# Two GNN layers on one core: set-up reordered, with extra transposes and all adjacency parts ordered by GpSimd

## The chip, the core and the metric

The kernel runs on one core of a Trainium2 chip. A core has five engines that run beside each other, each with its own queue of instructions in a fixed order: TensorE (PE, matrix products and transposes, results in PSUM), VectorE (DVE), ScalarE (ACT), GpSimd (POOL) and SyncE (SP, here only a queue that starts DMAs). They wait for each other by semaphores. The metric is the device time of one execution in microseconds, the median of several runs.

## What is computed

Eight graphs of 2048 nodes with 256 features share one 2048 × 2048 adjacency matrix of zeros and ones (int32). Layer 0 is attention with four heads over chunks of 256 keys, layer 1 a graph attention; both have a layer norm and a ReLU ahead and are added to their input.

```python
# layer 0, on h = relu(layernorm(x))
scores = einsum('bhnd,bhjcd->bhnjc', q, kc) / sqrt(Dh)      # 4 heads, 8 chunks of 256 keys
scores = clip(scores, -10.0, 10.0)
scores = where(mask == 0, -10.0, scores)                    # mask = adjacency
attn = softmax(scores, axis=-1)                             # within each chunk
ctx = einsum('bhnjc,bhjcd->bhnd', attn, vc)                 # summed over the chunks
x = x + layernorm(ctx @ Wo.T + bo + h) * gamma + beta
# layer 1, on h = relu(layernorm(x)) @ W
e = where(adj == 0, NEG_INF, leaky_relu(e_src[:, :, None] + e_dst[:, None, :]))
x = x + relu(softmax(e) @ h)
```

## The kernel before

Nodes are handled in blocks of 512 (`NB`; four blocks, `NNB`), each of four tiles of 128. For each graph, layer 0 runs 32 attention steps (`Attention.STEPS`: four blocks of queries, each with eight chunks of keys), and layer 1 follows. The order of all instructions is written out by hand; each engine takes its own in the order of the program. The set-up, which is what the change touches, runs once, ahead of the steps of the first graph.

**The adjacency matrix in the set-up.** The mask is kept in turned form as int8 bounds: clipping the logits from below by a constant and from above by a bound that is 80 or -80 does both the clip and the mask (`Attention.clip`, L530). To make the bounds, the matrix is read in 32 parts, each 128 rows of queries by half of the keys (1024 columns of int32, 512 KB). 24 of them (`nearest`, L1016) are done in the set-up, the other eight (`all_parts[-8:]`) beside the first attention steps. Each part passes through five stations:

- `load_rows` (L258): a DMA on SP's queue into one of four buffers (tile `rows`). The load of part i + 4 is issued after `find` of part i, L1031.
- `missing_of` (L267), called by `find`: VectorE compares with zero and writes bf16 (tile `z`), L277. A first half (`half` = 0) is written directly in the order of keys that the kernel uses. For a second half (`aside`, L271) VectorE writes in plain order, and GpSimd copies it into the other order, L281. `z` has five buffers, which it shares with the attention weights `e`.
- `turn_missing` (L284): eight transposes on TensorE into PSUM (`ps_z`), L292.
- `keep_bounds` (L295): ScalarE turns them into int8 bounds, L303. Blocks 0 and 1 (parts 0 to 15) stay in SBUF (`bounds[nb]`).
- Parts 16 to 23 (block 2) go to `bound_part` and from there to DRAM by a DMA that GpSimd issues at once, L306. `bound_part` has four tiles in turn (`part_tags`: r, o4, r, prod), so each tile is used twice in the set-up, and its second use waits until the first is landed.

`turn_missing` and `keep_bounds` together are `bound` (L1037).

**The projections in the set-up.** `proj.stats`, `power`, `shift` and `norm` make the normalised input of a block (VectorE, ScalarE), `turn` transposes it on TensorE (L375) and copies it to `hT` (L408 on VectorE, L410 on ScalarE), `qk` makes queries (part 0) and keys (part 1) of a block (L434; copied by ScalarE, L438), `values` its values (L448; L453 on VectorE). `turn_weight` transposes a weight (L250, L251). The set-up ends with `att.early(0)` to `early(3)`: logits of the first attention step and the first logits of the second (L490), clips (L530), exponentials (L539) and the first addition of exponentials, on GpSimd (L545). In the steps themselves, `begin` and `end` issue the products with the values (L506), the sums (L518) and the rest.

**PSUM.** Three rings of two tiles each: `s` (logits, and the projections of blocks 0 to 2), `n` and `t`, which take turns in the set-up (`ps_m`, `turn_missing`). A new tile of a ring waits until its forerunner but one has been read.

The lines that matter are these:

```python
for nb in range(NNB - 1):                 # L1047
    i = 6 * nb
    proj.qk(nb, 0, ps_h)
    find(i + 2, i + 3)
    bound(i, i + 1)
    proj.qk(nb, 1, ps_h)
    find(i + 4, i + 5)
    bound(i + 2, i + 3)
    proj.turn(nb + 1, 0)
    proj.values(nb)
    find(i + 6, i + 7)
    bound(i + 4, i + 5)
```

Of the kernel before, what the change touches and what calls it, by code (L numbers as in the profile page):

```python
# [17 lines left out]
P = 128  # L18
# [10 lines left out]
def gnn_two_layers(  # L29
# [18 lines left out]
    nc = tc.nc  # L48
# [7 lines left out]
    TB = NB // P  # L56
# [14 lines left out]
    def ps_n():  # L71
        return ps.tile([P, 512], F32, tag="n", name="ps_n")

    def ps_t():
        return ps.tile([P, 512], F32, tag="t", name="ps_t")
# [4 lines left out]
    def ps_m():  # L80
        if turn_about[0]:
            turn_about[1] += 1
            if turn_about[1] % 2:
                return ps_n()
        return ps_t()
# [9 lines left out]
    ident = const.tile([P, P], F32, name="ident")  # L95
# [19 lines left out]
    bound_d = [kept.tile([P, NT, NB], I8, name=f"bound_d{nb}") for nb in range(NNB)]  # L115
# [74 lines left out]
    def row_bcast(src, name):  # L190
        t = const.tile([P, F], F32, name=name)
        nc.sync.dma_start(t, row(src))
        return t
# [51 lines left out]
    def turn_weight(raw, wT):  # L245
        pt = ps_m()
        for di in range(FC):
            for do in range(FC):
                k = di * FC + do
                nc.tensor.transpose(pt[:, k * P:(k + 1) * P], raw[:, do, di * P:(di + 1) * P], ident)  # L250
        nc.vector.tensor_copy(wT.rearrange("p c f -> p (c f)"), pt)  # L251

    HALF = N // 2
    in_setup = [True]
# [3 lines left out]
    def load_rows(t, half):  # L258
        rows = xpool.tile([P, HALF], I32, tag="x", name="rows", bufs=NNB)
        of_block = adj[t // TB * NB:(t // TB + 1) * NB, half * HALF:(half + 1) * HALF]  # L260
        nc.sync.dma_start(rows, of_block.rearrange("(p t) k -> p t k", t=TB)[:, t % TB, :])
        return rows

    def in_blocks(keys):
        return keys.rearrange("p (k b t) -> p k t b", t=TB, b=Q)

    def missing_of(rows, t, half):  # L267

        tag = "e" if in_setup[0] else "hn"
        z = work.tile([P, 2 if in_setup[0] else 1, HALF], BF16, tag=tag, name="z", bufs=5)  # L270
        aside = in_setup[0] and half  # L271
        apart = dict(t=TB, b=Q)
        if aside:
            src, dst = rows, z[:, 1, :]
        else:
            src, dst = in_blocks(rows), z[:, 0, :].rearrange("p (k t b) -> p k t b", **apart)
        nc.vector.tensor_scalar(  # L277
            dst, src, 0.0, 0.0, op0=ALU.is_equal, op1=ALU.add, accum_out=missing[:, t, half:half + 1],
        )
        if aside:  # L280
            nc.gpsimd.tensor_copy(z[:, 0, :].rearrange("p (k t b) -> p k t b", **apart), in_blocks(z[:, 1, :]))  # L281
        return z[:, 0, :]

    def turn_missing(z):  # L284
        tag = "t"
        if turn_about[0]:
            turn_about[1] += 1
            if turn_about[1] % 2:
                tag = "n"
        pt = ps.tile([P, 8, P], BF16, tag=tag, name="ps_z")  # L290
        for k in range(8):
            nc.tensor.transpose(pt[:, k, :], z[:, k * P:(k + 1) * P], ident_b)  # L292
        return pt

    def keep_bounds(pt, t, half):  # L295

        nb, rows, cols = t // TB, slice(half * 8, (half + 1) * 8), slice((t % TB) * P, (t % TB + 1) * P)
        if nb in bounds:
            dst = bounds[nb][:, rows, cols]
        else:  # L300
            tag = part_tags[(2 * t + half) % 4] if in_setup[0] else "r"
            dst = work.tile([P, 8, P], I8, tag=tag, name="bound_part", bufs=2 if tag == "r" else 1)
        nc.scalar.activation(dst, pt, AF.Copy, scale=-2.0 * CLIP * SC, bias=CLIP * SC)  # L303
        if nb not in bounds:
            queue = nc.gpsimd if in_setup[0] else nc.scalar
            queue.dma_start(bound_d[nb][:, rows, cols], dst)  # L306

    def find_lone():
        nc.vector.tensor_reduce(lone, missing, AX.X, ALU.add)
# [4 lines left out]
    def adjacency(parts):  # L314


        def load(i):
            rows[i] = load_rows(*parts[i])

        def find(i):  # L320
            found[i] = missing_of(rows.pop(i), *parts[i])

        def turn(i):
            found[i] = turn_missing(found[i])

        def keep(i):
            keep_bounds(found.pop(i), *parts[i])

        finds = [9, 11, 15, 17, 21, 23, 29, 31]
        turns = [12, 12, 18, 18, 26, 26, 32, 32]  # L330
        todo = {}
        for i, (f, t) in enumerate(zip(finds, turns)):
            todo.setdefault(f - 6, []).append(lambda i=i: load(i))
            todo.setdefault(f, []).append(lambda i=i: find(i))
            todo.setdefault(t, []).append(pe(lambda i=i: turn(i)))
            todo.setdefault(t + 1, []).append(first(lambda i=i: keep(i)))
        return todo
# [122 lines left out]
    def fence(before, after):  # L460

        nop = nc.sync.nop()
        for x in before:
            tc.add_manual_dep(nop.ins, x.ins.name, SYNC, reason="both write one bank of PSUM")
        for x in after:
            tc.add_manual_dep(x.ins, nop.ins.name, SYNC, reason="both write one bank of PSUM")


    class Attention:
# [127 lines left out]
        def begin(self, f, pieces=()):  # L597

            self.run(pieces, "first")
            if self.has(f - 3):  # L600
                made = {}
                for kt in range(KT):
                    for half, c in ((0, 0), (1, 1)):
                        made.setdefault(c, []).extend(self.values(f - 3, half, c, kt))
                for c in range(2):
                    fence(self.before.pop((f - 3, c)), made[c])
            if self.has(f - 1):
                self.clip(f - 1, 0)
            if self.has(f - 3):
                self.invert(f - 3)  # L610
            if self.has(f - 2):
                self.exponentials(f - 2, 3)
            if self.has(f - 1):
                self.exponentials(f - 1, 0)
            self.run(pieces, "pe")
            if self.has(f - 1):
                for kt in range(KT):
                    self.logits(f - 1, 1, kt)
                    self.logits(f - 1, 2, kt)
            if self.has(f - 3):  # L620
                self.scale(f - 3, 0)
                self.scale(f - 3, 1)
            if self.has(f - 2):
                self.add(f - 2, 1)
            if self.has(f - 3):
                self.gather(f - 3)
            self.rest = pieces
# [377 lines left out]
    proj = Projection(0)  # L1005
# [9 lines left out]
    all_parts = [(t, half) for t in range(NT) for half in range(2)]  # L1015
    nearest = all_parts[:-8]  # L1016
    rows = {i: load_rows(*nearest[i]) for i in range(4)}
    proj.stats(0, range(TB))
    proj.power(0)
    turn_weight(raws["q"], wqT)  # L1020
    proj.shift(0)
    turn_weight(raws["k"], wkT)
    turn_weight(raws["v"], wvT)
    proj.norm(0, 0)
    proj.norm(0, 1)
    proj.load(2)
# [4 lines left out]
    def find(*parts):  # L1031
        for i in parts:
            found[i] = missing_of(rows.pop(i), *nearest[i])
            if i + 4 < len(nearest):
                rows[i + 4] = load_rows(*nearest[i + 4])

    def bound(*parts):  # L1037
        for i in parts:
            keep_bounds(turn_missing(found.pop(i)), *nearest[i])
# [4 lines left out]
    proj.power(1)  # L1044
    proj.shift(1)
    find(0, 1)
# [3 lines that stand above are left out]
        if nb == 0:  # L1050
            proj.norm(1, 0)
            proj.norm(1, 1)
            proj.load(3)
        find(i + 2, i + 3)
        bound(i, i + 1)
        proj.qk(nb, 1, ps_h)
        find(i + 4, i + 5)
        bound(i + 2, i + 3)
        if nb + 2 < NNB:
            proj.stats(nb + 2, range(TB))  # L1060
            proj.power(nb + 2)
            proj.shift(nb + 2)
        proj.turn(nb + 1, 0)
        proj.turn(nb + 1, 1)
        if nb + 2 < NNB:
            proj.norm(nb + 2, 0)
            proj.norm(nb + 2, 1)
        proj.values(nb)
        find(i + 6, i + 7)
        bound(i + 4, i + 5)  # L1070
        if nb == 0:
            bo_r = row_bcast(bo, "bo_r")
            gamma_r = row_bcast(gamma, "gamma_r")
            beta_r = row_bcast(beta, "beta_r")
    att = Attention(proj)
    att.early(0)
    proj.qk(NNB - 1, 0)
    att.early(1)
    find(20, 21)
# [2 lines left out]
    att.early(2)  # L1082
    bound(20, 21)
    find(22, 23)
    bound(22, 23)
    proj.values(NNB - 1)
    att.early(3)
    in_setup[0] = False

    def layer1_weight():  # L1090
# [27 lines left out]
    for b in range(B):  # L1118
# [205 lines left out]
        for i, (nb, j4) in enumerate(pieces1):  # L1324
# [34 lines left out]
            if ahead and i == len(pieces1) - 4:  # L1359
                att = Attention(ahead)  # L1360
# [38 lines left out]
```

## Time and profile before

| what | value |
|---|---|
| median of 3 runs | 3558.47 us (3555.39 to 3564.36) |
| the profiled execution | 3563.89 us |
| its span | 3562.1 us |
| granted clock, mean | 0.998 |
| L277 on VectorE, 24 parts, set-up | 1210 to 2184 ns |
| L281 on GpSimd, 12 copies, set-up | 1086 to 1133 ns |
| L292 on TensorE, 8 transposes of a part | 0.62 us |
| L303 on ScalarE, one part | 1.02 us |
| L306, one send on GpSimd's queue | 0.9 us, 2.7 to 9.7 us from issue to landing |
| rows, 512 KB, issue to landing | 5.4 us median |

Times within the execution count from the start of the span. The profile names each group by its line, engine, operation and tiles; "x8" is the number of instructions in it (an f32 matrix product shows as two). A figure in brackets is the time that the engine stood idle before, with what ended it. An instruction's duration on TensorE includes its latency, so a dense row of matmuls is best measured from the start of one group to the start of the next.

### The profile page before, as it was taken

Reading aid. Unit: us, or ns where it says so; the run is one execution under the profiler, and the core shown is the slowest. Engines: PE = TensorE matmul, PEld = TensorE weight load, DVE = VectorE, ACT = ScalarE, POOL = GpSimd, SP = SyncE. Lnnn points to the kernel's source line nnn. Section 1 sums busy time; section 2 is a strip of 40 time slices with the busy share of each in tenths; the row PEclk is TensorE's granted clock in tenths of the full one; section 3 lists DMA queues with packets and bytes.
Section 4 is the critical chain, followed back from the end, with each engine's and each line's share of the span. In section 5 each row is a group of like instructions: output and inputs, shape, how many; then the busy total and the mean of one; then the engine's idle time right before and its main releaser. Section 6 shows DMA issues by size and latency. Waiting matters only on the chain.

```text
span 3562.1 us, 104433 instructions
## 1 busy us (share of the span) xinstructions
PE 3527.6 (99%) x46080; PEld 2183.0 (61%) x46080; DVE 2639.0 (74%) x3979; ACT 1947.4 (55%) x2961; POOL 1808.9 (51%) x1182
## 2 busy tenths in 40 slices
PE   8999999999999999999999999999999999999999
PEld 5455785557755577555775557655586555855568
DVE  7888677867678676786767867678586785757866
ACT  6677426763267633676236762367624766147750
POOL 2688016870278702786037850378404784048731
PEclk9999999999999999999999999999999999999999
DMA  7545423444234441344423444234442434124321
GB/s 234 119 107 134 87 74 85 91 113 91 80 79 85 123 95 60 85 96 109 92 66 85 97 110 91 71 79 91 120 103 55 91 81 118 57 55 91 85 69 48
DMA packets 169111, 329.74 MB, mean 93 GB/s; under 512 B 35664, under 2 KB 97360, under 8 KB 160464
## 3 DMA queue, kind: packets, MB, share of 16 engines
q1 hardware_dynamic: 127696, 203.51, 19.2%
q0 software_dynamic: 32640, 118.50, 18.0%
q8 instruction: 360, 5.90, 0.7%
q10 hardware_dynamic: 8320, 1.05, 0.2%
q14 instruction: 95, 0.78, 0.1%
HBM read 154.14 MB, written 51.43 MB: 58 GB/s over the span
## 4 chain that ended last, share of the span: by engine, by line
PE 97%; DVE 1%; DMA 1%; ACT 1%; issue 0%; POOL 0%; ACTq 0%; DVEq 0%; POOLq 0%; SPq 0%
PE ps_s L490 25%; PE ps_n L506 24%; PE ps_s L963 12%; PE ps_t L518 7%; PE ps_n L963 6%; PE ps_t L963 6%; PE ps_t L714 2%; PE ps_t L434 2%; PE ps_n L434 2%; PE ps_s L434 2%; PE ps_t L814 2%; PE ps_n L814 2%; PE ps_t L448 1%; PE ps_n L448 1%; DVE z L277 0%
## 5 line engine op out<-in xcount | busy, mean ns | idle before, releaser
L530 DVE SCALAR_TENSOR_TENSOR e<-ps_s,bound 128x1024 f32<-128x1024 f32 x1024 | 1224.1, 1220 | 404.0 <-PE ps_s L490 400.6
L545 POOL TENSOR_TENSOR both<-e 128x1024 f32<-128x1024 f32 x512 | 1219.8, 2407 | 571.1 <-PE ps_t L518 355.6
L490 PE MATMUL ps_s<-q,k 64*32 64x512 f32 x16384 | 1431.8, 590 | 1.5 <-DVE e L530 1.4
L539 ACT ACTIVATE e<-e 128x1024 f32<-128x1024 f32 x1024 | 1050.6, 1050 | 481.1 <-DVE e L530 462.7
L506 PE MATMUL ps_n<-e,v 64*32 64x512 f32 x16384 | 1224.9, 591 | 2.4 <-DVE prod L560 2.4
L506 PEld LDWEIGHTS ps_n<-e,v 64*32 64x32 f32 x16384 | 460.9, 107 | 473.1 <-issue 384.1
L490 PEld LDWEIGHTS ps_s<-q,k 64*32 64x32 f32 x16384 | 459.5, 106 | 448.6 <-issue 331.2
L518 PE MATMUL ps_t<-both,ones 64*32 64x512 f32 x4096 | 537.9, 592 | 0.1
L963 PE MATMUL ps_s<-g,w 128*128 128x257 f32 x2048 | 447.8, 380 | 0.0
L963 PEld LDWEIGHTS ps_s<-g,w 128*128 128x128 f32 x2048 | 388.8, 190 | 56.3
L560 DVE TENSOR_TENSOR prod<-ps_n,rz 128x512 f32<-128x512 f32 x448 | 288.5, 686 | 162.8 <-PE ps_n L506 96.1
L986 POOL TENSOR_TENSOR x<-x,r 128x256 f32<-128x256 f32 x124 | 90.7, 745 | 466.2 <-ACT r L984 465.4
L946 DVE SCALAR_TENSOR_TENSOR w<-bound,w 128x1024 f32<-128x1024 int8 x256 | 314.7, 1229 | 8.7
L354 POOL TENSOR_TENSOR krn<-krn,mv 128x4 f32<-128x4 f32 x28 | 6.8, 242 | 575.4 <-DVE w L940 575.4
L963 PE MATMUL ps_n<-g,w 128*128 128x257 f32 x1024 | 292.4, 382 | 0.0
L963 PE MATMUL ps_t<-g,w 128*128 128x257 f32 x1024 | 289.7, 380 | 0.0
L550 ACT ACTIVATE rz<-ps_t 128x512 f32<-128x512 f32 x256 | 152.6, 596 | 229.4 <-PE ps_t L518 201.5
L940 DVE TENSOR_SCALAR w<-src,cd 128x512 f32<-128x512 f32 x512 | 263.1, 556 | 7.0 <-ACT src L921 6.6
L963 PEld LDWEIGHTS ps_n<-g,w 128*128 128x128 f32 x1024 | 192.8, 190 | 44.3 <-issue 17.6
L565 POOL DMA_DIRECT2D ctxT<-prod x224 | 191.0, 853 | 54.1 <-DVE prod L560 46.7
L963 PEld LDWEIGHTS ps_t<-g,w 128*128 128x128 f32 x1024 | 193.8, 189 | 28.2
L551 ACT ACTIVATE rz<-rz 128x512 f32<-128x512 f32 x256 | 161.4, 630 | 8.2
(133 smaller groups left out, 2910.4 us busy)
## 6 DMA issues: line engine op xcount, KB each, us to landing
ctxT<-prod POOLq DMA_DIRECT2D x224, 512.0 KB, 4.9
bound<-bound_d SPq DMA_DIRECT2D x62, 1024.0 KB, 6.2
turned_d<-squares SPq DMA_DIRECT2D x232, 128.0 KB, 2.4
hT<-turned_d SPq DMA_DIRECT2D x58, 512.0 KB, 4.3
rows<-in_adj_dram SPq DMA_DIRECT2D x32, 512.0 KB, 5.3
x<-in_x_dram SPq DMA_DIRECT2D x32, 512.0 KB, 4.9
out_dram<-x SPq DMA_DIRECT2D x31, 512.0 KB, 2.6
xp<-in_x_dram SPq DMA_DIRECT2D x28, 512.0 KB, 4.5
```

What stands on the lines that cost most here:

```text
L434: nc.tensor.matmul(in_key_order(pp) if i == 0 else pp, w[:, di, do * P:(do + 1) * P], h, start=di == 0, stop=di == FC - 1,)
L490: nc.tensor.matmul(self.s[n, o][c * Q:(c + 1) * Q, kt, :], self.k[p][rows, at:at + Q], self.q[p][rows, nb * NB:(nb + 1) * NB], start=True, ...
L506: made.append(nc.tensor.matmul(self.num[n, c][h * Q:(h + 1) * Q, :], self.v[rows, j * KT + kt, at:at + Q], self.e[n, p][rows, i * KT + kt, :],
L518: nc.tensor.matmul(self.total[n][h * Q:(h + 1) * Q, :], ones[rows, :], self.both[n, h // 2][rows, h % 2, :], start=half == 1, stop=half == 0,)
L530: nc.vector.scalar_tensor_tensor(self.e[n, p][:, i * KT:(i + 1) * KT, :], self.s.pop((n, o)), -CLIP * SC, bounds[nb][:, j * KT:(j + 1) * K ...
L539: nc.scalar.activation(e, e, AF.Exp, scale=1.0 / SC)
L545: nc.gpsimd.tensor_tensor(self.both[n, p], e[:, 0], e[:, 1], op=ALU.add)
L560: nc.vector.tensor_tensor(dst[:, c, :], self.num.pop((n, c)), self.rz[n], op=ALU.mult)
L565: nc.gpsimd.dma_start(self.ctxT[nb], self.prod.pop(n), accum_op=ALU.add)
L940: nc.vector.tensor_scalar(w[:, i, :], self.src[nb], self.cd[:, 0, j:j + 1], self.cd[:, 1, j:j + 1], op0=ALU.mult, op1=ALU.max,)
L946: nc.vector.scalar_tensor_tensor(two, bounds1[nb][:, j - 1:j + 1, :], 0.0, two, op0=ALU.is_gt, op1=ALU.mult)
L963: nc.tensor.matmul(accs[t][:, 0:F + 1], w[:, i, t * P:(t + 1) * P], g[:, j, :], start=j == 0, stop=j == NT - 1,)
```

## The change

The diff has five parts.

- `warm`: TensorE transposes the identity 16 times into a PSUM tile ahead of all else, and 8 times more behind the transposes of the weights. Nobody reads the results.
- The order of the set-up loop: for block 0, the keys' projection stands ahead of the bounds of parts 0 and 1, with `find(2, 3)` on VectorE ahead of it. After it, each `bound` follows two groups later than before relative to `find`; parts 16 and 17 are turned behind the first logits of attention.
- `aside` holds for all parts: VectorE writes each in plain order and GpSimd copies it into the order of the keys. This holds in the set-up alone; the eight later parts are as before.
- The sends of block 2's bounds are collected (`unsent`) and issued by `send_bounds`, which `find` calls behind its copies on GpSimd, and the set-up once at its end.
- `early(3)`, the second step's first logits, and their clip stand ahead of the last bounds and the last values; `begin` leaves that clip out when it has been done.

```diff
@@ missing_of
-        aside = in_setup[0] and half
+        aside = in_setup[0]
@@
+    unsent = []
+
+    def send_bounds():
+        while unsent:
+            nb, rows, cols, dst = unsent.pop(0)
+            nc.gpsimd.dma_start(bound_d[nb][:, rows, cols], dst)
+
@@ keep_bounds
-            queue = nc.gpsimd if in_setup[0] else nc.scalar
-            queue.dma_start(bound_d[nb][:, rows, cols], dst)
+            if in_setup[0]:
+                unsent.append((nb, rows, cols, dst))
+            else:
+                nc.scalar.dma_start(bound_d[nb][:, rows, cols], dst)
@@ begin
-            if self.has(f - 1):
+            if (f - 1, 0) in self.s:
                 self.clip(f - 1, 0)
@@ set-up
+    def warm(times):
+        pt = ps_m()
+        for k in range(times):
+            nc.tensor.transpose(pt[:, k % TB * P:(k % TB + 1) * P], ident, ident)
+
+    warm(16)
     proj.stats(0, range(TB))
     proj.power(0)
     turn_weight(raws["q"], wqT)
     proj.shift(0)
     turn_weight(raws["k"], wkT)
     turn_weight(raws["v"], wvT)
+    warm(8)
@@ find
             found[i] = missing_of(rows.pop(i), *nearest[i])
+        send_bounds()
+        for i in parts:
             if i + 4 < len(nearest):
                 rows[i + 4] = load_rows(*nearest[i + 4])
@@ loop
-        find(i + 2, i + 3)
-        bound(i, i + 1)
-        proj.qk(nb, 1, ps_h)
-        find(i + 4, i + 5)
-        bound(i + 2, i + 3)
+            find(2, 3)
+            proj.qk(0, 1, ps_h)
+            bound(0, 1)
+        else:
+            bound(i - 2, i - 1)
+            find(i + 2, i + 3)
+            proj.qk(nb, 1, ps_h)
+            bound(i, i + 1)
...
         proj.turn(nb + 1, 0)
         proj.turn(nb + 1, 1)
+        find(i + 4, i + 5)
...
         proj.values(nb)
+        bound(i + 2, i + 3)
         find(i + 6, i + 7)
-        bound(i + 4, i + 5)
@@ end of the set-up
     att.early(0)
+    bound(16, 17)
     proj.qk(NNB - 1, 0)
     att.early(1)
     find(20, 21)
...
     att.early(2)
     bound(20, 21)
     find(22, 23)
+    att.early(3)
+    att.clip(1, 0)
     bound(22, 23)
     proj.values(NNB - 1)
-    att.early(3)
+    send_bounds()
     in_setup[0] = False
```

## The prediction

> **What bounds the kernel now.** I read the page first (share of each engine, then the chain that ended last), then the busy time by stretch of the set-up, then the timeline of each engine there. The page:
>
> ```profile
> span 3562.1 us, 104433 instructions
> ...
> PE 3527.6 (99%) x46080; PEld 2183.0 (61%) x46080; DVE 2639.0 (74%) x3979; ACT 1947.4 (55%) x2961; POOL 1808.9 (51%) x1182
> ...
> PE 97%; DVE 1%; DMA 1%; ACT 1%; issue 0%; POOL 0%; ACTq 0%; DVEq 0%; POOLq 0%; SPq 0%
> ```
>
> TensorE is busy 99% and is 97% of the chain; idle are 34.6 us. The change touches the set-up only: compared instruction by instruction, the two programs have the same order on every engine from the first values of attention on. So only the first 86 us count. There, by stretch (time, then busy us of each engine and its instructions, clock, DMA share, GB/s):
>
> ```profile
> 28.00:58.00 30.00, 29.44 (x191) 19.75 (x190) 25.21 (x40) 21.14 (x32) 6.70 (x6) 1.00 0.71 225
> 58.00:72.00 14.00, 13.66 (x125) 6.24 (x122) 14.00 (x16) 9.40 (x12) 8.14 (x7) 1.00 0.76 235
> 72.00:76.00 4.00, 0.03 (x1) 0.04 (x2) 0.17 (x2) 1.65 (x2) 3.00 (x4) 0.93 0.99 302
> 76.00:86.00 10.00, 8.58 (x72) 5.43 (x80) 2.66 (x4) 4.05 (x4) 4.14 (x3) 0.86 0.39 130
> ```
>
> TensorE is full in the middle and loses time at both ends. Its own timeline (start, us, then the operation; the idle time before it in brackets):
>
> ```profile
> 5.29 1.09 PE L250 MATMUL ps_n<-ident,raw 128*128 128x128 f32 x4 [5.29 <-DMA raw<-in_L_gnn_Wq_dram]
> ...
> 11.20 5.07 PE L434 MATMUL ps_s<-hT,wqT 128*128 128x512 f32 x8
> ...
> 18.59 0.62 PE L292 MATMUL ps_z<-ident_b,z 128*128 128x128 bf16 x8 [1.71 <-POOL z L281]
> 19.05 3.65 PE L434 MATMUL ps_s<-hT,wkT 128*128 128x512 f32 x8
> ...
> 75.97 1.03 PE L292 MATMUL ps_z<-ident_b,z 128*128 128x128 bf16 x8 [4.25 <-POOL z L281]
> 76.80 2.96 PE L448 MATMUL ps_t<-wvT,hT 128*128 128x256 f32 x8
> 79.60 1.89 PE L448 MATMUL ps_n<-wvT,hT 128*128 128x256 f32 x8
> ...
> 84.75 1.49 PE L490 MATMUL ps_s<-q,k 64*32 64x512 f32 x20 [1.42 <-DVE e L530]
> ```
>
> The same eight projection matmuls take 5.07 us at 11.2 and 3.65 at 19.05; the same eight value matmuls 2.96 after the 4.25 us gap and 1.89 later: slow clock. Lost between 11.20 and the first values of attention (85.67), start to start against the same group elsewhere: slow first projection 1.6; the wait for adjacency part 1 at 18.59, 1.9; two smaller waits for GpSimd, 0.4 and 0.5; the gap before part 23, 4.6; the slow clock after it, 1.4; the wait for clip(1,0), 1.9. Sum 12.3 us: the most this change can win there. What ends the large gap:
>
> ```profile
> 70.88 1.29 DVE L277 TENSOR_SCALAR_CACHE_REDUCE z<-rows 128x1024 bf16<-128x1024 int32 x1
> ...
> 73.03 1.80 POOL L306 DMA_DIRECT2D bound_d<-bound_part  x2 [0.89 <-ACT bound_part L303]
> 74.83 1.09 POOL L281 COPY z<-z 128x1024 bf16<-128x1024 bf16 x1
> ...
> 76.61 1.02 ACT L303 ACTIVATE bound_part<-ps_z 128x1024 int8<-128x1024 bf16 x1 [2.96 <-DMA bound_d<-bound_part]
> ...
> 78.70 1.02 ACT L303 ACTIVATE bound_part<-ps_z 128x1024 int8<-128x1024 bf16 x1 [1.07 <-DMA bound_d<-bound_part]
> 79.62 1.05 ACT L539 ACTIVATE e<-e 128x1024 f32<-128x1024 f32 x1
> ```
>
> VectorE is done with part 23 at 72.1, but its copy stands on GpSimd's queue behind the sends of parts 20 and 21. ScalarE's last bounds wait for a tile that the sends of parts 18 and 19 still hold.
>
> **What the Trainium skill says.** "TensorE: Matmul & The Clock Gate", Part 1: the array runs at half rate until a free-running window of about 3.4 us was busy, and falls back after an idle one. The trace agrees (5.07 against 3.65; 2.96 after the gap). Part 4 there says that transposes do not count as busy in the same way, which would leave the new transposes without effect. The trace speaks against it, without proof: from 51.8 to 55.2 about half of TensorE's time is transposes (L292, L375), and the clock stays full. "SBUF — State Buffer", Who interferes with whom: a VectorE instruction with one SBUF input outside its two-port modes doesn't contend with GpSimd. All 12 copies of before took 1.09 to 1.13 us beside VectorE's work. "DMA: Bandwidth & Descriptors", Issuing engines are not separate DMA queues: GpSimd's sends share the 16 DMA engines with all else. The trace agrees: a send lands 8.5 and 9.7 us after issue at 68 to 69 us, beside 2 MB of stores and 1 MB of rows, and 2.7 to 3.1 at 78 to 80.
>
> **Part by part.** Times are in the frame of the profiled execution.
>
> *Transposes of the identity.* 16 before Wq lands: the identity is ready at 1.44; at 0.88 us for four (6.17 − 5.29, slow clock) 16 take 3.5, to about 5.2. They lie in idle time. Then the turns of the weights follow nearly without a gap, so that the clock should rise at about 7.4, not near 14. The 8 more end at 8.6 if fast, 9.6 if slow. The normalised tiles come from ScalarE at 8.46 to 9.94, so the fast case costs nothing; the slow one delays the last transposes by some 0.4. Fast: hT is there 0.25 earlier, the first projection starts at 10.95 and takes 3.49 as at 19.05, to 14.4 (before 16.3). Bounds: +0.4 (no warming) to −2.0; I take −1.9.
>
> *Keys of block 0 ahead of parts 0 and 1.* TensorE runs on at 14.6 (0.2 for ScalarE freeing the bank) to 18.1. Parts 0 and 1 are copied by then: VectorE starts at 14.1, 1.14 each, and GpSimd adds 1.13 and a hand-over of 0.2, to 17.8. The 1.9 wait goes.
>
> *All parts through GpSimd.* VectorE's pass falls from 1.91 to 1.14 us (start to start) for 12 parts, −9.2 us; GpSimd copies 12 more, +13.4. Per pair, the second part is ready 2 × 1.14 + 0.2 + 1.13 = 3.6 us after VectorE starts, against 1.91 + 1.14 + 1.3 = 4.4. With bound two groups behind find, I followed all 24 parts: TensorE's work from 10.95 to the end of part 23 is 8 half projections × 3.49 + 12 pairs of parts × 0.9 + 3 turns × 0.96 + 3 values × 3.55 + logits 4.7 = 57 us, to about 68.1; no part is later than this order needs it. Rows are loaded four ahead and land in 5.4 us (median); VectorE frees them at 1.14 a part, so that DMA has 0.5 to 2 us to spare. SP's queue has the same order; VectorE reaches part 19 at 55.0, so the last rows are issued there (61.3 before), and Wo, W1, the two 1 MB stores and two later rows behind them move up by 6.3 us too.
>
> *The sends.* send_bounds puts 16 and 17 behind the copies of 20 and 21 (GpSimd 61.0 to 62.8), then add(0,0) (exponentials done at 61.9; 2.4 us, to 65.2), then the copies of 22 and 23, then the sends of 18 to 21. Part 23 on VectorE waits for a z tile that TensorE frees with part 20 (65.8), so its copy ends at 68.2 and sends 18 and 19 go out at 68.2 and 69.1. Nothing is queued ahead of the copies any more: the 4.6 us gap and its slow clock go. But part_tags has four tiles: ScalarE's parts 20 and 21 wait for the landing of 16 and 17, parts 22 and 23 for 18 and 19; behind them on ScalarE stands the exponential of (0,3), which TensorE's values(0) need. Landing relative to the last rows: 16 and 17 go out where 18 and 19 did before, so 8.5 to 9 us: 69.0 and 70.9. 18 and 19 go out where 20 and 21 did (6.9, 6.5), a little later: 5.2 to 5.5, so 73.7 and 74.3. Not shown by the trace; bounds 2.7 and 9.7.
>
> *End.* values(3) needs the banks of parts 20 and 21: ScalarE frees them at 70.1 and 71.9, so TensorE waits 1.9 and ends at 73.7; logits(1,0) and clip(1,0) have been moved ahead (clip done at 68.4), so that the 1.9 wait goes; logits(1,1) and (1,2) end at 75.6. ScalarE: part 22 to 74.8, 23 to 75.8, exponential (0,3) to 76.9. The third values matmul starts at 77.0 instead of 85.8; GpSimd's add(0,1) behind the last send (77.0 to 79.4) comes just in time for the sums. Ledger: −12.3 − 0.25 + 0.2 + 1.9 + 1.2 + 0.1 = **−9.1**; by the two clock readings −8.8. I take −9.0: the execution would take 3563.9 − 9.0 = 3554.9. The median of the three runs is 5.4 below that execution: 3558.5 − 9.0 = **3549.5**.
>
> **Rivals.**
> *The transposes don't warm the array.* For: Part 4, and the window 7.4 to 10.8, mostly transposes, is followed by a slow one. Against: that window has gaps of 0.3. All up to part 20 is 2.3 later: −6.7, 3551.8.
> *The sends land late (8.5 and 9.7 us, as 18 and 19 did).* Part 23 at 79.8, the exponential at 80.9: −4.9, 3553.6. Against: the stores are through by then.
> *They land in 3 us.* Then parts 20 to 23 run one behind the other and TensorE waits 2 us at most: −10.5 to −12, 3547.
> *GpSimd becomes the bound (slower).* VectorE's contiguous pass may hold up the copy, beside which only the strided one and small operations were seen. GpSimd then has 15.4 + 24 c + 4.2 (two sends, one add) to the end of copy 23, and 8.8 from there to values(0). Even at c = 2.4 us; that is the time of its f32 add (2.38). At 2.9 us: 98.0, +12, 3570.5. Against: 12 copies at 1.12.
>
> **Numbers.** Forecast 0.5, no warming 0.15, late landing 0.1, early landing 0.2, GpSimd bound 0.05. About 0.3% (10.7 us) is what a measurement of this kernel can tell from no change; the three runs lie 9 us apart, so a median is uncertain by some 3. Over the line on the fast side: 0.4 of the forecast, three quarters of early landing, a quarter of no warming, a tenth of late: 0.40. Slower: 0.06 with the noise. Same: 0.54. The range takes in early landing and late landing with 3 us of noise: 3543 to 3557.
>
> **What would show it.** The first eight projection matmuls in 3.6 us; no gap over 0.5 us on TensorE from 11 to 66; 24 copies of 1.1 us; ScalarE's parts 20 to 23 waiting for DMA at 69 to 76; values(0) at about 77. Wrong would be: a projection of 5 us; copies over 2 us; rows that VectorE waits for between 30 and 55.

## The result and the profile after

The changed kernel took 3547.36 us (median of 6 runs, 3543.44 to 3550.16), the kernel before beside it 3558.54 us (6 runs): a ratio of 0.9966, 95% interval 0.9953 to 0.9979. That is 12 us less, with 5 on either side. Two more comparisons of the same pair gave 0.9962 (0.9949 to 0.9974) and 0.9961 (0.9949 to 0.9974), 13.5 and 13.9 us. The forecast was 9.0 us less. The profiled execution took 3548.53 us, 15.4 less than the one of before; 5.4 of that are the distance of before's execution from its own median, so it isn't read as the effect.

The page of the changed kernel, the lines that answer to those of before:

```profile
span 3546.8 us, 104495 instructions
...
PE 3522.0 (99%) x46104; PEld 2184.4 (62%) x46104; DVE 2632.2 (74%) x3979; ACT 1946.5 (55%) x2961; POOL 1822.2 (51%) x1194
...
PE 97%; DVE 1%; ACT 1%; DMA 0%; issue 0%; POOL 0%; ACTq 0%; DVEq 0%; POOLq 0%
```

TensorE is idle for 24.8 us (3546.8 − 3522.0) instead of 34.6. It is busy 5.6 us less, although 24 transposes came in (x46104 against x46080): a slow clock shows as busy time. VectorE has 6.8 us less, GpSimd 13.3 more: the copies of 12 parts changed engines. The same stretches of the set-up (time, then busy us of PE, PEld, DVE, ACT, POOL and their instructions, clock, DMA share, GB/s):

```profile
28.00:58.00 30.00, 30.00 (x223) 19.97 (x222) 22.93 (x44) 21.83 (x31) 14.75 (x14) 1.00 0.81 254
58.00:72.00 14.00, 13.37 (x117) 6.88 (x116) 8.24 (x12) 9.11 (x11) 11.50 (x10) 1.00 0.89 283
72.00:76.00 4.00, 3.72 (x40) 1.77 (x40) 0.94 (x2) 0.57 (x1) 0.89 (x1) 1.00 0.72 207
76.00:86.00 10.00, 8.58 (x116) 2.65 (x120) 4.56 (x5) 6.52 (x9) 5.50 (x4) 1.00 0.27 57
```

The stretch from 72 to 76 us, in which TensorE had done 0.03 us of work, is now 3.72 us full, and the clock is full throughout. TensorE's timeline:

```profile
1.50 3.68 PE L1030 MATMUL ps_n<-ident 128*128 128x128 f32 x16 [1.50 <-POOL ident masks.py:199]
5.25 1.02 PE L250 MATMUL ps_t<-ident,raw 128*128 128x128 f32 x4
6.11 0.60 PE L250 MATMUL ps_n<-ident,raw 128*128 128x128 f32 x4
...
11.08 3.70 PE L443 MATMUL ps_s<-hT,wqT 128*128 128x512 f32 x8 [0.35 <-DVE hT L417]
14.62 3.67 PE L443 MATMUL ps_s<-hT,wkT 128*128 128x512 f32 x8
18.13 1.06 PE L292 MATMUL ps_z<-ident_b,z 128*128 128x128 bf16 x16
...
69.27 1.95 PE L457 MATMUL ps_t<-wvT,hT 128*128 128x256 f32 x8
71.84 1.99 PE L457 MATMUL ps_n<-wvT,hT 128*128 128x256 f32 x8 [0.63 <-ACT bound_part L310]
73.77 1.95 PE L499 MATMUL ps_s<-q,k 64*32 64x512 f32 x32
77.42 2.45 PE L515 MATMUL ps_n<-e,v 64*32 64x512 f32 x26 [1.71 <-ACT bound_part L310]
...
87.76 0.61 PE L515 MATMUL ps_n<-e,v 64*32 64x512 f32 x4
```

Four transposes of a weight fall from 1.02 to 0.60 us after nothing but transposes: the clock rose on them. The first projection takes 3.70 us instead of 5.07, parts 0 and 1 follow the keys with no wait, the 4.25 us gap is gone, and 0.63 and 1.71 us of waits are left. The first values of attention (L515) start at 77.42 instead of 85.67. The last line is the mark for all that follows: **the second step's first values**, from which on the order of work is the same in both kernels. It stands at 87.76 us, 7.2 earlier than before:

```profile
94.94 0.61 PE L506 MATMUL ps_n<-e,v 64*32 64x512 f32 x4
```

ScalarE's timeline says where the two waits come from:

```profile
67.58 1.02 ACT L310 ACTIVATE bound_part<-ps_z 128x1024 int8<-128x1024 bf16 x1 [0.22 <-DMA bound_d<-bound_part]
...
70.77 1.02 ACT L310 ACTIVATE bound_part<-ps_z 128x1024 int8<-128x1024 bf16 x1 [2.16 <-DMA bound_d<-bound_part]
...
75.43 1.94 ACT L310 ACTIVATE bound_part<-ps_z 128x1024 int8<-128x1024 bf16 x2 [3.64 <-DMA bound_d<-bound_part]
77.25 3.90 ACT L548 ACTIVATE e<-e 128x1024 f32<-128x1024 f32 x4
```

Three of its last four parts wait for earlier sends to land; the fourth ("x2" are two parts) follows the third at once. GpSimd's:

```profile
67.54 1.14 POOL L281 COPY z<-z 128x1024 bf16<-128x1024 bf16 x1 [0.99 <-DVE z L277]
68.57 2.66 POOL L300 DMA_DIRECT2D bound_d<-bound_part  x3
72.08 0.89 POOL L300 DMA_DIRECT2D bound_d<-bound_part  x1 [0.85 <-ACT bound_part L310]
76.75 1.80 POOL L300 DMA_DIRECT2D bound_d<-bound_part  x2 [3.78 <-ACT bound_part L310]
78.56 2.40 POOL L554 TENSOR_TENSOR both<-e 128x1024 f32<-128x1024 f32 x1
```

Its last two sends wait for ScalarE's last parts, and the addition stands behind them, to 80.96; TensorE's first sums need it, and its loads of weights for them stand idle for 0.8 us until it is done.

### The profile page after: what moved, and what is told of

The parts are those of the page before. It is cut to its first block, busy times and chain, and to the rows that moved or that the text cites. A ratio compares the mean times of both kernels' runs of the same rounds, so it can differ in the third digit from the quotient of the medians.

```text
span 3546.8 us, 104495 instructions
## 1 busy us (share of the span) xinstructions
PE 3522.0 (99%) x46104; PEld 2184.4 (62%) x46104; DVE 2632.2 (74%) x3979; ACT 1946.5 (55%) x2961; POOL 1822.2 (51%) x1194
## 3 DMA queue, kind: packets, MB, share of 16 engines
q0 software_dynamic: 32640, 118.50, 18.1%
## 4 chain that ended last, share of the span: by engine, by line
PE 97%; DVE 1%; ACT 1%; DMA 0%; issue 0%; POOL 0%; ACTq 0%; DVEq 0%; POOLq 0%
PE ps_s L499 25%; PE ps_n L515 24%; PE ps_s L972 13%; PE ps_t L527 7%; PE ps_n L972 6%; PE ps_t L972 6%; PE ps_t L723 2%; PE ps_t L443 2%; PE ps_n L443 2%; PE ps_s L443 2%; PE ps_t L823 2%; PE ps_t L457 2%; PE ps_n L823 2%; PE ps_n L457 2%; PE ps_z L292 0%; PE ps_t L701 0%
## 5 line engine op out<-in xcount | busy, mean ns | idle before, releaser
L515 PE MATMUL ps_n<-e,v 64*32 64x512 f32 x16384 | 1219.3, 590 | 3.9 <-DVE prod L569 2.2
L515 PEld LDWEIGHTS ps_n<-e,v 64*32 64x32 f32 x16384 | 463.1, 107 | 472.5 <-issue 393.0
```

What stands on the lines that cost most here:

```text
L515: made.append(nc.tensor.matmul(self.num[n, c][h * Q:(h + 1) * Q, :], self.v[rows, j * KT + kt, at:at + Q], self.e[n, p][rows, i * KT + kt, :],
```

## The experiments

Where nothing else is said, they are the changed kernel with one edit. Marks are those of the timelines; the expectations count the same marks from 0.24 us earlier, so their numbers are 0.24 larger. The gain at the mark is against 95.12 us, the mean of two traces of before (94.94, 95.30). "By time" is the ratio, taken of 3558.5 us; the half width of an interval is 2 to 5 us. The experiments ran on three chips (A, B, C): comparisons inside one are the closer ones. The three experiments on A have no changed kernel beside them; it is compared from the first row, whose chip isn't recorded, and from B and C.

| kernel (chip) | mark us | gain at mark | median us (runs) | ratio and 95% interval | by time |
|---|---|---|---|---|---|
| changed kernel | 87.76 | 7.4 | 3547.36 (6) | 0.9966, 0.9953 to 0.9979 | 12.1 |
| before again (A) | 95.30 | | 3560.68 (12) | 0.9995, 0.9986 to 1.0003 | 1.8 |
| without the identity's transposes (A) | 88.83 | 6.3 | 3551.34 (20) | 0.9972, 0.9966 to 0.9979 | 10.0 |
| before, with these transposes (A) | 95.31 | −0.2 | 3560.51 (12) | 1.0002, 0.9994 to 1.0010 | −0.7 |
| eight tiles (A) | 83.30 | 11.8 | 3544.13 (5) | 0.9952, 0.9938 to 0.9965 | 17.1 |
| changed kernel again (B) | 85.95 | 9.2 | 3547.46 (5) | 0.9962, 0.9949 to 0.9974 | 13.5 |
| sends at once (B) | 89.63 | 5.5 | 3553.17 (12) | 0.9981, 0.9972 to 0.9989 | 6.8 |
| second halves alone by GpSimd (B) | 89.42 | 5.7 | 3549.82 (6) | 0.9974, 0.9963 to 0.9985 | 9.3 |
| second step's logits last (B) | 87.56 | 7.6 | 3552.91 (12) | 0.9977, 0.9968 to 0.9985 | 8.2 |
| changed kernel, third time (C) | 85.99 | 9.1 | 3549.82 (5) | 0.9961, 0.9949 to 0.9974 | 13.9 |
| eight tiles again (C) | 83.18 | 11.9 | 3543.96 (5) | 0.9946, 0.9933 to 0.9958 | 19.2 |
| eight tiles, second halves alone (C) | 84.73 | 10.4 | 3548.79 (5) | 0.9959, 0.9945 to 0.9972 | 14.6 |
| eight tiles, second step's logits last (C) | 86.36 | 8.8 | 3547.99 (5) | 0.9955, 0.9942 to 0.9967 | 16.0 |

### The transposes of the identity, taken out and put in alone

Does a transpose warm the array, and what is that worth without the new order?

```diff
@@ changed kernel, without
-    warm(16)
...
-    warm(8)
```

> The changed kernel without both groups of transposes of the identity. Theory (they raise the clock early): the first eight projection matmuls take about 5.1 us again instead of 3.6, and the second step's first values come 1.5 to 2.3 us later than in the changed kernel, at 89.5 to 90.3 us instead of 88.0; the time rises by about 2 us, to some 3549.5. Rival (transposes do not count as busy, the clock would have been up anyway): projection 3.6 us, values at 88.0, no difference.

TensorE's timeline of the kernel without them:

```profile
6.21 1.06 PE L250 MATMUL ps_t<-ident,raw 128*128 128x128 f32 x4
...
11.17 4.92 PE L443 MATMUL ps_s<-hT,wqT 128*128 128x512 f32 x8
15.93 3.60 PE L443 MATMUL ps_s<-hT,wkT 128*128 128x512 f32 x8
```

The four transposes stay at 1.06 us, the first projection at 4.92, and the keys start 1.3 us later than 14.62. The mark stands 1.1 to 2.9 us later than in the three traces of the changed kernel; the gain that is left there, 6.3 us, is near the 6.7 that the prediction gave for "no warming". By time 10.0 us are left, 2 to 4 less than with the transposes, with intervals that overlap. So the transposes do warm the array. Put into the kernel before, alone:

```diff
@@ before, with
+    warm(16)
     proj.stats(0, range(TB))
...
     turn_weight(raws["v"], wvT)
+    warm(8)
```

> The kernel before with both groups of transposes and nothing else of the change. Theory: the first projection falls from 5.07 to about 3.6 us, but TensorE then waits for the GpSimd copy of part 1, which VectorE starts no earlier, until 18.6 us as before; the second step's first values stay at 95.2 within 0.3 and the time at the 3558.5 of before within 0.1%. Rival 1: the gain carries through, 93.3 to 94 us. Rival 2 (the two further PSUM tiles shift the rings and make all that follows faster): values at 95.2, but the rest some 4 us shorter than that of before, 3554.

```profile
6.68 0.66 PE L250 MATMUL ps_t<-ident,raw 128*128 128x128 f32 x4
...
11.03 5.40 PE L434 MATMUL ps_s<-hT,wqT 128*128 128x512 f32 x8 [0.35 <-DVE hT L408]
18.68 0.62 PE L292 MATMUL ps_z<-ident_b,z 128*128 128x128 bf16 x8 [1.71 <-POOL z L281]
```

The weights are turned fast (0.66), but the clock falls again in this trace: the granted clock is 0.50 from 11.4 to 14.9 us. Between lie four single transposes with gaps of 0.16 to 0.23 us, as in the traces in which it doesn't fall. The 1.71 us wait for part 1 stands as before, and the time is that of before (1.0002), so the two further PSUM tiles alone speed up nothing behind the mark. In this trace the warming wasn't kept; what it would be worth in the old order once kept isn't shown. Of the eleven traces with the transposes nine have a first projection of 3.70 us and two of 5.40 us; the three without have 4.92 to 5.56 us. "TensorE: Matmul & The Clock Gate" of the Trainium skill says in Part 1 that the window is free-running, so that what decides is how a busy stretch falls on it. The two misses agree with that: in both the clock is 0.50 for the same 3.4 us, after the same instructions as in the nine. Part 4, which says that transposes leave the clock low, is contradicted by the traces here (1.02 and then 0.60 us, with transposes alone before).

### Where the last parts are held: eight tiles instead of four

The prediction put most of what is left on the four tiles that the sends hold. Each of the eight sends gets its own:

```diff
@@ keep_bounds
-    part_tags = ["r", "o4", "r", "prod"]
+    part_tags = ["r", "o4", "r", "prod", "ctx", "rz", "ctx", "mean"]
+    part_bufs = {"r": 2, "ctx": 2}
...
-            tag = part_tags[(2 * t + half) % 4] if in_setup[0] else "r"
+            tag = part_tags[(2 * t + half) % 8] if in_setup[0] else "r"
...
```

> The changed kernel with eight tiles for the bounds of block 2 instead of four, so that no second use waits for a landing. Theory (ScalarE's waits for the sends of parts 16 to 19 hold back the last values and the exponential of (0,3)): ScalarE's waits for DMA go, the last values run through, attention's first values start at about 74.8 us instead of 77.4 and the second step's at 84.3 to 85 instead of 88.0; time 3.0 to 3.7 us below the changed kernel, about 3544. Rival (the end of the set-up is held by GpSimd's queue or by the clock): 87 to 88 us, no difference.

TensorE's timeline with eight tiles:

```profile
69.40 1.95 PE L458 MATMUL ps_t<-wvT,hT 128*128 128x256 f32 x8
71.18 1.89 PE L458 MATMUL ps_n<-wvT,hT 128*128 128x256 f32 x8
73.00 1.95 PE L500 MATMUL ps_s<-q,k 64*32 64x512 f32 x32
74.75 1.92 PE L516 MATMUL ps_n<-e,v 64*32 64x512 f32 x32
...
83.30 0.61 PE L516 MATMUL ps_n<-e,v 64*32 64x512 f32 x4
```

No wait is left in that stretch, the mark falls to 83.30, and the time is below that of both kernels. Once more beside the changed kernel:

> The kernel with eight tiles for block 2's bounds once more, beside the changed kernel on the same chip. If the 3.3 us between their medians are those of the landings, the second step's first values stand at 83.5 +- 0.6 us again, and the median is 2.5 to 4 us under that of the changed kernel. The rival is the spread of the medians: then the difference is anything from 0 to 5 us while the trace shows the same 83.5.

> The changed kernel, unaltered, as the neighbour of the three others. Its second step's first values are expected between 86.2 and 88.0 us, its median 11 to 14 us below that of before.

The marks came as expected (83.18 and 85.99). The medians lie 5.9 us apart, more than the expected 2.5 to 4 and than the 2.8 us of the marks, though the intervals overlap. The landing of the sends did cost the changed kernel 2.7 to 4.5 us at the mark.

### Three other parts of the change taken back

The sends, the copies on GpSimd and the place of the second step's logits were each taken back. The order of the set-up loop was not: that it removes the wait for part 1 is read from the timelines, and what it is worth alone isn't shown. The changed kernel again, as their neighbour on chip B:

> The changed kernel once more. In the first traces the set-up gives 7.2 us (second step's first values at 88.0 instead of 95.2 us), the medians 11 to 13. Theory (the rest is chance of few runs and of the pair of traces): ratio 0.9980, a gain of 7 to 8 us, second step's values at 88.0 within 0.5. Rival (what follows the set-up is also faster, by some 4 us): ratio 0.9966 again, a gain of 12 us, with the values at 88.0.

First the sends, back behind each part:

```diff
@@ keep_bounds
-                unsent.append((nb, rows, cols, dst))
+                nc.gpsimd.dma_start(bound_d[nb][:, rows, cols], dst)
```

> The changed kernel, but each send issued right behind its part, as before the change. Theory (the sends in front of the copies are what held up part 23): sends 20 and 21 stand ahead of the copies of 22 and 23 again, TensorE waits about 4 us for part 22 near 68 us and runs slowly behind it; the second step's first values at 88.7 to 90.5 us, time 1 to 2 us above the changed kernel. Rival (collecting the sends only makes the landings later and ScalarE wait): 85 to 88 us, no slower or faster than the changed kernel.

```profile
72.11 2.06 PE L292 MATMUL ps_z<-ident_b,z 128*128 128x128 bf16 x16 [3.08 <-POOL z L281]
73.97 3.71 PE L457 MATMUL ps_t<-wvT,hT 128*128 128x256 f32 x8
```

The copies of the last parts stand behind the sends again: TensorE waits 3.08 us, and works on at the slow clock (3.71 instead of 1.95). The mark is 3.7 us later than its neighbour's, the time 6.7 us longer by the ratios. Of the 3.7 us, 0.6 aren't the edit's: the keys start at 15.20 instead of 14.59, since VectorE waits 0.48 us for rows of the input x until 11.5. Next, only second halves through GpSimd:

```diff
@@ missing_of
-        aside = in_setup[0]
+        aside = in_setup[0] and half
```

> The changed kernel, but only second halves ordered by GpSimd, as before the change; VectorE writes the first halves in key order, 0.77 us more for each of 12. Theory (in the new order VectorE has time to spare, TensorE is the bound to 66 us, and part 23 waits for its z tile): second step's first values at 88.0 within 0.7, the time within 1.5 us of the changed kernel. Rival (VectorE's 9 us were what the change saved): TensorE waits for parts from 30 us on, values at 90 to 95.

TensorE's timeline, then ScalarE's:

```profile
73.79 3.68 PE L457 MATMUL ps_t<-wvT,hT 128*128 128x256 f32 x8 [3.75 <-ACT bound_part L310]
```

```profile
72.71 1.02 ACT L310 ACTIVATE bound_part<-ps_z 128x1024 int8<-128x1024 bf16 x1 [4.74 <-DMA bound_d<-bound_part]
```

TensorE waits for no part on the way (once 0.42 us for VectorE's `hT`): slower passes of VectorE still keep up. But the sends of parts 16 and 17 go out at 63.29 instead of 60.85, the first of them lands after 9.3 us (8.6 in the neighbour), and ScalarE waits 4.74 us for it; the slow clock follows. The mark is 3.5 us later than the neighbour's, the time 4.2 us longer; of the two theories neither gave this wait. At the mark the two edits cost about the same (3.1 and 3.5 us), and their intervals by time overlap: which part gives more isn't shown. With eight tiles there is no landing to wait for:

> With eight tiles, and only the second halves ordered by GpSimd, as in before. Theory: what the second halves alone cost (1.7 us at the mark) was a later landing of the sends of parts 16 and 17, so with eight tiles it is gone: the second step's first values at 83.5 +- 0.7 us, the median within 1 us of eight tiles alone. Rival: VectorE's slower passes (1.9 us instead of 1.2 for 12 parts) make the last parts themselves late: 85 to 86 us, the median 1.5 to 3 us above.

```profile
11.03 5.40 PE L444 MATMUL ps_s<-hT,wqT 128*128 128x512 f32 x8 [0.35 <-DVE hT L418]
16.27 3.60 PE L444 MATMUL ps_s<-hT,wkT 128*128 128x512 f32 x8
...
76.18 1.92 PE L516 MATMUL ps_n<-e,v 64*32 64x512 f32 x32
```

In this trace the first projection is slow (granted clock 0.50 from 11.5 to 14.9 us); VectorE has begun no part when it starts, so that isn't the edit's doing. From the keys to the first values it takes 59.9 us, as with eight tiles alone (14.63 to 74.63, 60.0): the mark's 1.6 us are the clock, and the edit costs nothing there. The median is 4.8 us above eight tiles alone, with intervals that overlap; 3 us of that aren't explained. Last, the second step's logits back behind the last values, and their clip back in the step:

```diff
-    att.early(3)
-    att.clip(1, 0)
     bound(22, 23)
     proj.values(NNB - 1)
+    att.early(3)
```

> The changed kernel with the second step's first logits behind the last values again and their clip in the step. Theory (TensorE waits for the parts 22 and 23 and for ScalarE's landings anyway, so the place of these logits is hidden): attention's first values at 77.4 to 78, the second step's at 88.0 within 0.5, no difference in time. Rival (the moved logits save the 1.9 us wait for their clip): values at 79.3 and 89.9, 1.9 us slower.

> With eight tiles, and the second step's first logits back behind the last values, their clip in the second step. Theory: with four tiles this cost nothing since TensorE waited for the bounds' landing anyway; with eight it is full from 69 us on, so the wait for the clip (1.4 us) is bare: second step's first values at 84.9 +- 0.5 us. Rival: the order of these two doesn't matter there either: 83.5 +- 0.4.

TensorE's timeline of the second, with eight tiles:

```profile
68.78 0.62 PE L293 MATMUL ps_z<-ident_b,z 128*128 128x128 bf16 x8 [1.46 <-POOL z L282]
...
76.18 1.49 PE L500 MATMUL ps_s<-q,k 64*32 64x512 f32 x20 [1.42 <-DVE e L540]
```

The expected wait for the clip is there (1.42), and a second one of 1.46, for GpSimd's copy of the last part: the 1.9 us of logits had covered that too. The mark is 3.2 us later, against 1.4 expected. With four tiles it was 87.56, as late as the first trace of the changed kernel but 1.6 later than that of its own chip; of these, 0.7 us come from late rows of x again (VectorE waits 0.72 us for them, the keys start at 15.29). Its trace has the same two waits, 1.47 and 1.42 us. So with four tiles the place of these logits isn't free either: about 0.9 us, where no difference was expected.

## Why the prediction was right

**The mechanism held, nearly step by step.** Warming: the keys started at 14.62 us, forecast 14.6, and ended at 18.1, forecast 18.1. The clock rose earlier than the 7.4 of the forecast (four transposes took 0.60 at 6.11), and at different moments in different executions. The wait for part 1 went. All 24 copies took about 1.1 us, which removes the slower rival. TensorE was full from 11 to 67 us. VectorE waited once for rows (0.85 us at 30.2, where the forecast had 0.5 to 2 us to spare), which delayed nobody; it issued the last rows at 55.4, forecast 55.0. Copy 23 ended at 68.6, forecast 68.2. ScalarE's last parts waited for landings, and the first values started at 77.42; the 77.0 of the forecast is the start of the third of them, which came at 78.4.

**Terms of the sum that were mis-sized.** "Logits 4.7" in TensorE's work is 0.9 short: the three groups took 1.88, 1.88 and 1.86 us, the last of them with half the matmuls, so that part 23 was turned at 69.27 instead of 68.1. This cost nothing, since it only shortened the next wait. "ScalarE frees them at 70.1 and 71.9, so TensorE waits 1.9": part 20 could start 1.4 us earlier than put, at 67.58, part 21 freed its bank for 71.84, as put, and TensorE's idle time was 0.63; in the two other traces 1.27 and 1.32. "18 and 19 ... 73.7 and 74.3": send 18 held part 22 until 75.4, 1.7 us later, and part 23 came behind it. So the first two values waited for the bank that part 23 gives back, and the third stood 0.8 us more for the exponential of (0,3), the wait that the prediction named. "add(0,1) behind the last send (77.0 to 79.4) comes just in time for the sums", put at 0.1: it ended at 80.96 instead of 79.4, and the sums' loads waited 0.8 us for it. With these two waits the gain shrank from 8.25 us at the first values to 7.2 at the mark.

In the other two traces sends 16 and 17 landed 8.6 to 9.7 us after issue and 18 and 19 after 4.6 to 5.0, near the 8.5 to 9 and 5.2 to 5.5 of the forecast (6.6 to 8.7 and 6.5 to 6.8 in the first), and the gain at the mark was 9.2 and 9.1. The forecast, 9.0, lies among the three (7.4, 9.2, 9.1). That it lies so near is in part luck: the work of TensorE was put too short by about as much as the wait behind it was put too long, and the landing of one send moves by 2 us between traces of one kernel.

**What the prediction didn't have.** By time the gain is 12.1, 13.5 and 13.9 us, by the marks 8.6 on the mean. 4 to 5 us come behind the mark, where both kernels have the same order. Each interval alone would allow nearly as little as the marks; three comparisons on the same side make it likely that something is there. The traces have about as much on the mean (3.9 us), but that is less than they differ among themselves: from the mark to the end the two of before take 3461.2 and 3467.2 us and the one with the transposes alone 3464.1, the three of the changed kernel 3459.0, 3459.8 and 3462.0. No single place holds it. One such place can be shown, in the last attention step of before:

```profile
3409.04 3.68 PE L506 MATMUL ps_n<-e,v 64*32 64x512 f32 x32 [1.44 <-DVE prod L560]
```

and with eight tiles, second run:

```profile
3392.53 2.52 PE L516 MATMUL ps_n<-e,v 64*32 64x512 f32 x32 [0.87 <-DVE prod L570]
```

The granted clock was 0.50 from 3410.3 to 3417.1 us in the first and 1.00 in the second; from these values to the next layer's first product it takes 9.47 us and 6.60; these 2.9 us are half of the 6 us by which the two traces of before differ. But neither the wait nor the old set-up decides it: the second trace of before has a wait of 1.42 us there and the third of the changed kernel one of 1.92, both with 6.60 us at the full clock. Whether an earlier start lets the later work fall better on the clock's windows or on the transfers, the runs don't tell; it stays open. So does why "second step's logits last" is 5.3 us slower than its neighbour by time and 1.6 at the mark.

## What to carry to other kernels

A queue in which an engine issues transfers that wait for late results, and then does work that others need, should have that work ahead of the waits: taking back this one reordering cost about 3 us, and where it was not applied, at the addition behind the last sends, a part of the gain was lost. Where buffers are refilled behind a transfer, ask for its landing under the load of that moment, and whether idle tiles elsewhere can end the question: four more tile names gave about as much here as the best of the reorderings. A block of work moved ahead can cover more than one wait, so undo it in the kernel in which nothing else covers them before calling it worthless.

## What was not expected of the hardware

f32 transposes alone raised TensorE's clock: after 16 of them, 0.22 us each, and four of a weight (1.02 us), the next four took 0.60. The moment of the rise differs between traces of one kernel: the first four transposes of a weight took 1.02, 0.66 and 1.11 us in the three traces of the changed kernel, the second four 0.60, 0.66 and 0.93. In two of eleven traces the clock fell again before the first projection. After an idle stretch of 3.08 us the next sixteen transposes took 2.06 us instead of 1.07 and eight matmuls 3.71 instead of 1.95; after one of 3.75 us eight matmuls took 3.68. So these two waits cost another 2.7 and 1.7 us in slow clock.
